# Layer-norm scaling on GpSimd, odd operand shapes for small VectorE steps, three small steps a chunk: a two-layer cross-attention block on Trainium2

## The chip, the cores and the metric

The kernel runs on one core of a Trainium2 chip. The metric is device time in microseconds (us), the median of three runs. The engines of the core are TensorE (PE, with PEld for its weight loads), VectorE (DVE), ScalarE (ACT), GpSimd (POOL) and SyncE (SP, which issues nearly all DMAs here). Each engine works through its own instructions in program order. What one engine needs of another is guarded by semaphores: an instruction that waits holds up everything behind it on its engine.

## The reference

Two transformer layers on x (4 sequences of 512 rows, 320 wide) with a context of 4 x 1601 rows, 192 wide; 20 heads of 16:

```python
def layer(x, context, heads=20):
    h1 = _ln(x, n1_g, n1_b)
    x = _attn(h1, h1, q1, k1, v1, o1_w, o1_b, heads) + x
    h2 = _ln(x, n2_g, n2_b)
    x = _attn(h2, context, q2, k2, v2, o2_w, o2_b, heads) + x
    h3 = _ln(x, n3_g, n3_b)
    a, g = jnp.split(h3 @ ff_w1 + ff_b1, 2, axis=-1)
    return a * jax.nn.gelu(g, approximate=False) @ ff_w2 + ff_b2 + x

def _ln(x, g, b):
    m = jnp.mean(x, axis=-1, keepdims=True)
    v = jnp.mean(jnp.square(x - m), axis=-1, keepdims=True)
    return (x - m) * jax.lax.rsqrt(v + EPS) * g + b
```

All is float32. There are three norms a layer for each of the four sequences, 24 in all.

## The kernel before, in words

**Units and chunks.** The work is cut into units: for each layer first self-attention, then cross-attention, for each sequence b and each group g of four heads (5 groups), and at last a feed-forward unit for each sequence. An attention unit goes over its keys in chunks of 128: 4 chunks in self-attention (512 keys), 13 in cross-attention (1601 keys). In a chunk, `main` lets PE compute the scores of four heads into PSUM banks (`st`, L1210), subtract the rows' maxima by one more matmul (L1213, from the row `m`), ACT take the exponential (L1223) into one of a ring of buffers, and, a chunk later, PE multiply with the values (`av`, L1237). ACT copies that to SBUF (L1253), and POOL adds it to the unit's output `o` (L1254), one add a chunk.

**Maxima.** The next unit's maxima are found in the same chunks: PE computes its scores once more with queries in the partitions (`sps`, L1024), and DVE reduces each bank of 512 keys to one column (L1043, `pm` or `nmax`; L1062 for the rest of the keys). `max_reduce` (L1079) joins the columns of a cross unit. `max_end` splits the 16 maxima into a rounded part and a remainder (L1089 and L1090, into the tile `nm`), transposes them on DVE (L1091) and sends them with four DMAs into the row `m`. All this shares the eight PSUM banks: a bank that DVE has not yet read holds up the matmul which is to have it next.

**Norms.** `add_norm` puts the steps of a norm into a chain. For each 128 rows t of four, `stats(t)` computes mean and variance on DVE (L530, L531) into `mv`. `root` computes the reciprocal square root of the four variances: a first guess by integer arithmetic (`guess_root`, L494 to L498 on DVE, L500 on POOL), then three Newton steps (`better_root`, L507 to L510, on POOL) in two calls. `normalise(t)` is L546: (x - mean) * rstd into `hn`, by one DVE tensor-scalar instruction with two column operands, 320 wide; in a feed-forward norm a second one, 64 wide, writes a copy of the last columns. `turn(k)` transposes `hn` on PE (L559), ACT applies gain and bias (L566), and POOL adds the bias row of the coming projection to x (L572), which may not happen before `hn` has been made from x. The first norm of all is done while `start["on"]` is true, with its root on DVE.

**What orders the work.** Chains of small jobs (norms, projections, values, splits of queries and keys) are kept in queues with costs and due times. After the matmuls of each chunk `steps` runs jobs from them. A job of cost `LIGHT` (a `stats`, the first part of `root`, a `normalise`, a transposition of context, a reciprocal) is run only while `clock["lights"]` lasts: `lights` is the number of such jobs in one call, two a chunk, or one in the last chunk of a unit and in chunks with extra maxima; one in feed-forward units. Two rounds of the clock pass in a chunk. `root` step 1, `normalise(0)` and `turn(0)` each ask for a round after the step before. `see` adds an instruction to the model by which PSUM banks are chosen (class `Pace`).

**Queries and keys.** The projected queries and keys are copied by ACT and, in cross-attention, DVE to a staging tile; POOL splits them into a rounded part and a remainder (`split`, L700 and L701), and two rounds later SP moves them to where the matmuls read them.

Of the kernel before, what the change touches and what calls it, by code (L numbers as in the profile page):

```python
# [9 lines left out]
F32 = mybir.dt.float32  # L10
F32R = mybir.dt.float32r
I32 = mybir.dt.int32
AF = mybir.ActivationFunctionType
ALU = mybir.AluOpType
# [9 lines left out]
P = 128  # L24
NQ = N // P
G, HG = 5, 4
GD = HG * DH
SLOT = 32
# [98 lines left out]
def kernel(ctx: ExitStack, tc: tile.TileContext, x, context, ws, out):  # L127
# [18 lines left out]
    nc = tc.nc  # L146
    dma = nc.sync.dma_start

    const = ctx.enter_context(tc.tile_pool(name="const", bufs=1))
# [26 lines left out]

    nmax = [const.tile([P, HG * NQ], F32, name=f"nmax{i}") for i in range(2)]
    kbuf = [const.tile([P, 4 * QT + P], F32, name=f"kT{i}") for i in range(4)]  # L180
    qbuf = [const.tile([P, 2, 2, N // 2], F32, name=f"q{i}") for i in range(4)]

# [307 lines left out]

    def guess_root(var):

        a, h, y, z = (two.tile([P, NQ], F32, tag=f"root{i}", name=f"root{i}") for i in range(4))
        see(nc.vector.tensor_scalar(a, var, EPS, None, ALU.add))  # L494
        see(nc.vector.tensor_scalar(
            z.bitcast(I32), a.bitcast(I32), 1, None, ALU.logical_shift_right
        ))
        see(nc.vector.tensor_scalar(y.bitcast(I32), z.bitcast(I32), -1, 0x5F3759DF, ALU.mult, ALU.add))  # L498
        eng = nc.vector if start["on"] else nc.gpsimd
        eng.tensor_scalar(h, a, -0.5, None, ALU.mult)  # L500
        return h, y, z
# [8 lines left out]
        eng.tensor_tensor(y, y, z, ALU.mult)  # L510

    hn_used = []


    readers = []
# [5 lines left out]
    def add_norm(l, b, i, put, done, due):  # L521
        xb = xs[b]
        s = {}

        def stats(t):
            if t == 0:
                hn_used.append(b)
                s["mv"] = two.tile([P, NQ, 2], F32, tag="mv", name="mv")
            st = three.tile([P, 6], F32, tag="st6", name="st6")
            see(nc.vector.bn_stats(st, xb[:, t, :]))  # L530
            see(nc.vector.bn_aggr(s["mv"][:, t, :], st))  # L531

        def root(step):
            if step == 0:
                s["root"] = guess_root(s["mv"][:, :, 1])
                s["rstd"] = s["root"][1]
            for _ in range(step + 1):
                better_root(*s["root"])
            s["round"] = clock["round"]

        def normalise(t):
            if t == 0:
                s["hn"] = one.tile([P, NQ, D + REST], F32, tag="hn", name="hn")

            for to, at, n in ((0, 0, D), (D, D - REST, REST))[: 1 + i // 2]:
                see(nc.vector.tensor_scalar(  # L546
                    s["hn"][:, t, to : to + n], xb[:, t, at : at + n],
                    s["mv"][:, t, 0:1], s["rstd"][:, t : t + 1], ALU.subtract, ALU.mult,
                ))
            s["round"] = clock["round"]  # L550

        def turn(k, at, n):
            if k == 0:
                s["hT"] = two.tile([P, 3, N], F32, tag="hT", name="hT")
                readers.append(done)
            ps = step_bank([P, N], "hps")
            n += REST if n == REST else 0
            for t in range(NQ):
                see(nc.tensor.transpose(ps[:n, t * P : (t + 1) * P], s["hn"][:, t, at : at + n], ident))  # L559
            if start["on"] and k == 1:  # L560
                see(nc.vector.tensor_scalar(
                    s["hT"][:n, k, :], ps[:n, :],
                    lng[i][:n, k : k + 1], lnb[i][:n, k : k + 1], ALU.mult, ALU.add,
                ))
            else:
                see(nc.scalar.activation(  # L566
                    s["hT"][:n, k, :], ps[:n, :], AF.Identity,
                    bias=lnb[i][:n, k : k + 1], scale=lng[i][:n, k : k + 1],
                ))
            for t in ((0,), (1,), (2, 3))[k]:  # L570

                nc.gpsimd.tensor_tensor(xb[:, t, :], xb[:, t, :], brow[(3 * l + i) % 2], ALU.add)  # L572
            if k == 2:
                hn_used.pop()
                put(s["hT"])

        for t in range(NQ):
            add(
                "norm", LIGHT, lambda t=t: stats(t), due - 22 + t,
                (lambda: stage[b] == 3 * l + i and not hn_used and b in loaded) if t == 0 else yes,  # L580
                (lambda: b == 0 or clock["round"] >= loaded[b] + 5) if t == 0 else yes,
            )
        for step in range(2):
            add(
                "norm", 0.0 if step else LIGHT, lambda step=step: root(step), due - 18 + step, yes,
                (lambda: clock["round"] > s["round"]) if step else yes,
            )
        for t in range(NQ):
            add(
                "norm", LIGHT, lambda t=t: normalise(t), due - 13 + t, yes,  # L590
                (lambda: clock["round"] >= s["round"] + 1) if t == 0 else yes,
            )
        for k, at, n in (DK if i < 2 else FK + [(2, 2 * P, REST)]):
            add(
                "norm", 0.58, lambda k=k, at=at, n=n: turn(k, at, n), due - 6 + 2 * k,
                may_overwrite if k == 0 else yes, lambda: clock["round"] >= s["round"] + 1,
            )
# [413 lines left out]
    def max_pairs(u):  # L1011

        full = u.nkeys // 512
        rest = u.nkeys - full * 512
        ns = full + (1 if rest else 0)
        u.nm = nmax[u.n % 2]
        u.pm = two.tile([P, NQ, HG, ns], F32, tag="pm", name="pm") if ns > 1 else None

        def passes(heads, outs, t, keys):

            def one_pass(e):
                for j, out in zip(heads, outs):
                    rows = slice(j * SLOT, (j + 1) * SLOT)
                    see(nc.tensor.matmul(  # L1024
                        out,
                        lhsT=u.q[rows, t // 2, e, t % 2 * P : (t % 2 + 1) * P].bitcast(F32R),
                        rhs=u.kT[rows, keys].bitcast(F32R),
                        start=(e == 0),
                        stop=(e == 1),
                    ))  # L1030

            return [lambda e=e: one_pass(e) for e in range(2)]

        def full_two(heads, t, s):
            pss = [bank("sps") for _ in heads]
            if ns == 1:
                to = u.nm.rearrange("p (j t) -> p j t", t=NQ)[:, :, t]
            else:
                to = u.pm[:, t, :, s]

            def reduce():
                for j, ps in zip(heads, pss):
                    see(nc.vector.tensor_reduce(to[:, j : j + 1], ps, AX.X, ALU.max, negate=(ns == 1)))  # L1043

            keys = slice(u.k0 + s * 512, u.k0 + (s + 1) * 512)
            return passes(heads, pss, t, keys), reduce

        def rest_two(heads):

            w = rest + rest % 2  # L1050
            pss = [bank("sps") for _ in heads]
            todo = [
                f
                for t in range(NQ)
                for f in passes(
                    heads, [ps[:, t * w : (t + 1) * w] for ps in pss], t, slice(u.nkeys - w, u.nkeys),
                )
            ]

            def reduce():  # L1060
                for j, ps in zip(heads, pss):
                    see(nc.vector.tensor_reduce(  # L1062
                        u.pm[:, :, j, full], ps[:, : NQ * w].rearrange("p (t w) -> p t w", w=w), AX.X, ALU.max
                    ))

            return todo, reduce

        pairs = [
            deque([lambda heads=heads, t=t, s=s: full_two(heads, t, s)] for s in range(full) for t in range(NQ))
            for heads in ((2, 3), (0, 1))  # L1070
        ]
        if rest:
            for q, heads in zip(pairs, ((2, 3), (0, 1))):
                q.append([lambda heads=heads: rest_two(heads)])
        return pairs
# [6 lines left out]

    def max_end(u):

        both = two.tile([P, SLOT], F32, tag="nm2", name="nm2")
        turned = two.tile([P, SLOT], F32, tag="turned", name="turned")
        high, low = (both.rearrange("p (j e t) -> p e j t", j=HG, e=2)[:, e] for e in range(2))
        nm = u.nm.rearrange("p (j t) -> p j t", t=NQ)
        see(nc.vector.tensor_scalar(high.bitcast(F32R), nm, 1.0, None, ALU.mult))  # L1089
        see(nc.vector.tensor_tensor(low, nm, high, ALU.subtract))  # L1090
        see(nc.vector.transpose(turned, both))  # L1091
        to = u.mrow.rearrange("(n s) (t i r) -> s i n t r", s=DH, t=NQ, r=SLOT)[0]
# [104 lines left out]
    def main(u, give, nxt):  # L1197
# [60 lines left out]
        for c in range(u.nch):  # L1258
# [15 lines left out]
                round_of([], extra[0])  # L1274
            flush()
            late.append(lambda c=c: values(c))
            steps(None, 1 if extra or c == u.nch - 1 else 2)
            for i, e in enumerate(extra[1:]):
                if i and next_cost() is not None:
                    run(pick())  # L1280
# [303 lines left out]
```

## Time and profile before

| | |
|---|---|
| median of 3 runs | 3002.72 us (3000.33 to 3009.86) |
| the profiled execution, its own time | 2998.76 us |
| span of its instructions | 2997.0 us |
| mean granted TensorE clock | 0.996 |
| POOL adds of `o` (L1254), two largest groups | 359 x 1283 ns, 191 x 1283 ns |
| maxima on DVE (L1043), two groups | 1920 x 682 ns, 640 x 682 ns |

How to read it: the page and the views of the trace give one execution. A group's row is: line, engine, operation, output and inputs by their names, shapes, count; then busy time in us and mean ns of one; then the idle time of the engine just before these instructions, with what ended it. A row with a line's instructions gives shortest, median and longest duration in ns, and first and last start. A row of the timeline begins with the start and the duration in us; in brackets stands the idle time before it. In a row of stretches the columns are the stretch, its length, the busy us (and instructions) of PE, PEld, DVE, ACT and POOL, then the granted clock, the share of DMA and its GB/s.

### The profile page before, as it was taken

How to read it: one execution, taken by the hardware profiler on the slowest of the kernel's cores; microseconds unless marked ns; L12 is line 12 of the kernel's file. 1: busy time of each engine (PE TensorE's matmuls, PEld its weight loads, DVE VectorE, ACT ScalarE, POOL GpSimd, SP SyncE). 2: the span in 40 equal slices, each digit the busy share in tenths (PEclk: the TensorE clock that was granted, in tenths of full speed). 3: DMA queues.
4: the chain of work that ended last, by engine and by line, in shares of the span. 5: the costliest groups of instructions: out<-in, count | busy, mean ns of one | idle time of the engine just before them, and what ended most of it. 6: DMA issues, size and time to landing. Idle time of an engine off the chain costs nothing. (4 is left out here: it accounts for less than half of the span.)

```text
span 2997.0 us, 92121 instructions
## 1 busy us (share of the span) xinstructions
PE 2918.5 (97%) x37842; PEld 1605.1 (54%) x37842; DVE 2054.5 (69%) x4011; ACT 1955.5 (65%) x4029; POOL 1325.0 (44%) x1499
## 2 busy tenths in 40 slices
PE   8999999999999999999999999999999999999999
PEld 4455555555555555455554555555555555544555
DVE  7777878788888788322257778788878877873221
ACT  4777577887887888511147775778878878884101
POOL 3556454555455554201125563555654554541100
PEclk9999999999999999999999999999999999999999
DMA  4434221222132121300124332221221221212000
GB/s 113 120 98 113 71 70 44 64 70 58 43 76 60 34 65 28 111 7 0 32 51 100 106 87 64 65 65 32 71 58 36 54 69 38 56 36 74 14 10 14
DMA packets 221150, 178.00 MB, mean 59 GB/s; under 512 B 137652, under 2 KB 175416, under 8 KB 220728
## 3 DMA queue, kind: packets, MB, share of 16 engines
q1 hardware_dynamic: 219928, 171.05, 22.2%
q8 instruction: 297, 4.87, 0.7%
q14 instruction: 125, 1.02, 0.1%
q10 hardware_dynamic: 800, 1.06, 0.1%
HBM read 54.67 MB, written 29.56 MB: 28 GB/s over the span
## 5 line engine op out<-in xcount | busy, mean ns | idle before, releaser
L1043 DVE TENSOR_REDUCE pm<-sps 128x1 f32<-128x512 f32 x1920 | 1191.9, 682 | 108.3 <-PE sps L1024 101.5
L1024 PE MATMUL sps<-kT,q 32*128 32x512 f32 (+1 forms) x6400 | 1059.0, 402 | 18.2 <-DMA q<-stage 6.2
L1223 ACT ACTIVATE pr<-st 128x512 f32<-128x512 f32 (+1 forms) x1710 | 904.8, 603 | 189.4 <-PE st L1213 179.5
L1210 PE MATMUL st<-q,kT 32*128 32x512 f32 (+1 forms) x5440 | 921.6, 433 | 2.9 <-DVE pm L1043 1.3
L1254 POOL TENSOR_TENSOR o<-o,pr 128x512 f32<-128x512 f32 x359 | 460.5, 1283 | 642.9 <-ACT pr L1253 632.0
L1210 PEld LDWEIGHTS st<-q,kT 32*128 32x128 f32 (+1 forms) x5440 | 476.8, 180 | 353.8 <-ACT pr L1223 142.1
L1237 PE MATMUL av<-pr,vals 128*32 128x512 f32 (+1 forms) x3420 | 635.3, 607 | 31.3 <-DVE pm L1043 8.4
L1024 PEld LDWEIGHTS sps<-kT,q 32*128 32x128 f32 x6400 | 547.6, 184 | 119.8 <-DVE pm L1043 19.2
L1213 PE MATMUL st<-m,units 32*128 32x512 f32 (+1 forms) x2720 | 529.6, 390 | 0.8 <-DMA m<-turned 0.8
L1223 ACT ACTIVATE wself<-st 128x512 f32<-128x512 f32 (+1 forms) x867 | 462.8, 603 | 83.3 <-PE st L1213 79.6
L1043 DVE TENSOR_REDUCE nmax<-sps 128x1 f32<-128x512 f32 x640 | 396.8, 682 | 124.0 <-PE sps L1024 120.2
L1237 PE MATMUL av<-wself,vals 128*32 128x512 f32 (+1 forms) x1734 | 369.7, 605 | 12.3 <-DVE pm L1043 5.3
L1254 POOL TENSOR_TENSOR o<-o,wself 128x512 f32<-128x512 f32 x191 | 245.0, 1283 | 291.7 <-ACT wself L1253 288.7
L1332 PE MATMUL fps<-hT,w 128*128 128x512 f32 x640 | 283.7, 597 | 0.0
L1355 ACT ACTIVATE pr<-fps,b 128x512 f32<-128x512 f32 x80 | 54.8, 688 | 345.9 <-PE fps L1345 245.3
L1213 PEld LDWEIGHTS st<-m,units 32*128 32x128 f32 (+1 forms) x2720 | 249.0, 180 | 19.8 <-POOL stage L700 1.2
L1253 ACT COPY pr<-av 128x512 f32<-128x512 f32 x359 | 219.0, 610 | 25.1 <-PE av L1237 24.9
L1332 PEld LDWEIGHTS fps<-hT,w 128*128 128x128 f32 x640 | 118.8, 190 | 149.4 <-issue 148.5
L1237 PEld LDWEIGHTS av<-pr,vals 128*32 128x32 f32 (+1 forms) x3420 | 91.3, 108 | 199.2 <-DVE pm L1043 109.7
L700 POOL TENSOR_SCALAR stage<-stage 128x256 fp32r<-128x256 f32 (+1 forms) x155 | 106.5, 687 | 141.3 <-ACT stage L850 75.2
L500 POOL TENSOR_SCALAR root<-root 128x4 f32<-128x4 f32 x23 | 5.2, 224 | 298.2 <-DVE root L494 298.0
L885 PEld LDWEIGHTS kps<-ctxT,w 32*128 32x128 f32 (+1 forms) x4992 | 113.2, 162 | 43.3 <-ACT pr L1223 21.2
(99 smaller groups left out, 3161.3 us busy)
## 6 DMA issues: line engine op xcount, KB each, us to landing
q<-stage SPq DMA_DIRECT2D x157, 256.0 KB
kT<-w SPq DMA_DIRECT2D x120, 208.0 KB
outs<-o SPq DMA_DIRECT2D x80, 256.0 KB
kT<-stage SPq DMA_DIRECT2D x78, 128.0 KB
aT<-outs SPq DMA_DIRECT2D x32, 224.0 KB
oturn<-over SPq DMA_DIRECT2D x32, 224.0 KB
kT<-w SPq DMA_DIRECT2D x40, 144.0 KB
w<-in_L_xattn_ff_w_dram SPq DMA_DIRECT2D x20, 256.0 KB
```

The lines of the kernel that those rows point to most:

```text
L700: eng.tensor_scalar(high.bitcast(F32R), x, 1.0, None, ALU.mult)
L885: see(nc.tensor.matmul(ps[to : to + n, :PIECE], lhsT=wk_q[rows, k, u.g * GD : u.g * GD + n], rhs=first.kvT[rows, k, at : at + PIECE], star ...
L1024: see(nc.tensor.matmul(out, lhsT=u.q[rows, t // 2, e, t % 2 * P : (t % 2 + 1) * P].bitcast(F32R), rhs=u.kT[rows, keys].bitcast(F32R), star ...
L1043: see(nc.vector.tensor_reduce(to[:, j : j + 1], ps, AX.X, ALU.max, negate=(ns == 1)))
L1210: see(nc.tensor.matmul(st[:r, :], lhsT=keys, rhs=u.q[rows, :, e].bitcast(F32R), start=(e == 0), stop=False))
L1213: see(nc.tensor.matmul(st[:r, :], lhsT=units_of[rows, :r].bitcast(F32R), rhs=u.mrow[rows, :].bitcast(F32R), start=False, stop=True,))
L1223: see(nc.scalar.activation(p[:r], st[:r], AF.Exp))
L1237: see(nc.tensor.matmul(ps[j * SLOT : (j + 1) * SLOT, :], lhsT=columns_of[:r, head : head + SLOT], rhs=pr.pop((c, j))[:r, :], start=True, s ...
L1253: see(nc.scalar.copy(vo, ps))
L1254: nc.gpsimd.tensor_tensor(u.o, u.o, vo, ALU.add)
L1332: see(nc.tensor.matmul(ps, lhsT=w1[:, k, i * FF + c * P : i * FF + (c + 1) * P], rhs=u.hT[:, k, :], start=ahead and k == 0, stop=not ahead ...
L1355: see(nc.scalar.activation(gl, pss[1], AF.Gelu, bias=b1[:, NHC + c : NHC + c + 1]))
```

## The change

`normalise` issues its instruction on POOL instead of DVE, save for the first norm, and the instruction no longer goes through `see`. The tiles of the root get other shapes: three of them are views of 3 x 2 elements in a tile of 3 x 3, the fourth is 6 elements without a gap; `mv` becomes two fixed tiles with two more columns, set to 1 once at the start. So the root is taken of six values, of which four are used. The first step of `max_end` now reads 20 elements in one row, the 16 maxima and four zeros that are set once, and writes 5 groups of 4 apart from each other, in a room 8 elements wider. `steps` is called with three light jobs a chunk where it was two. No DMA is added or taken away.

```diff
-    nmax = [const.tile([P, HG * NQ], F32, name=f"nmax{i}") for i in range(2)]
+    nmax = [const.tile([P, (HG + 1) * NQ], F32, name=f"nmax{i}") for i in range(2)]
+    for nm in nmax:
+        nc.gpsimd.memset(nm[:, HG * NQ :], 0.0)
...
-        a, h, y, z = (two.tile([P, NQ], F32, tag=f"root{i}", name=f"root{i}") for i in range(4))
+        a, h, y = (two.tile([P, 3, 3], F32, tag=f"root{i}", name=f"root{i}")[:, :, :2] for i in range(3))
+        z = two.tile([P, 6], F32, tag="root3", name="root3").rearrange("p (a b) -> p a b", b=2)
...
+    mvs = [const.tile([P, 6, 2], F32, name=f"mv{i}") for i in range(2)]
+    for mv in mvs:
+        nc.gpsimd.memset(mv[:, NQ:], 1.0)
...
-                s["mv"] = two.tile([P, NQ, 2], F32, tag="mv", name="mv")
+                mvs.reverse()
+                s["mv"] = mvs[0]
...
-                s["rstd"] = s["root"][1]
+                s["rstd"] = [s["root"][1][:, t // 2, t % 2 : t % 2 + 1] for t in range(NQ)]
...
-                see(nc.vector.tensor_scalar(
+                these = (
                     s["hn"][:, t, to : to + n], xb[:, t, at : at + n],
-                    s["mv"][:, t, 0:1], s["rstd"][:, t : t + 1], ALU.subtract, ALU.mult,
-                ))
+                    s["mv"][:, t, 0:1], s["rstd"][t], ALU.subtract, ALU.mult,
+                )
+                if start["on"]:
+                    see(nc.vector.tensor_scalar(*these))
+                else:
+                    nc.gpsimd.tensor_scalar(*these)
...
-        u.nm = nmax[u.n % 2]
+        u.nmax = nmax[u.n % 2]
+        u.nm = u.nmax[:, : HG * NQ]
...
-        both = two.tile([P, SLOT], F32, tag="nm2", name="nm2")
+        room = two.tile([P, SLOT + 2 * NQ], F32, tag="nm2", name="nm2")
+        both = room[:, :SLOT]
...
-        see(nc.vector.tensor_scalar(high.bitcast(F32R), nm, 1.0, None, ALU.mult))
+        apart = room.rearrange("p (j e t) -> p e j t", j=HG + 1, e=2)[:, 0]
+        see(nc.vector.tensor_scalar(apart.bitcast(F32R), u.nmax, 1.0, None, ALU.mult))
...
-            steps(None, 1 if extra or c == u.nch - 1 else 2)
+            steps(None, 1 if extra or c == u.nch - 1 else 3)
```

## The prediction

> **What bounds the kernel now.** I read the busy times first, then the same by stage, then who makes TensorE (PE) wait, then the groups of VectorE (DVE) and GpSimd (POOL).
>
> ```profile
> span 2997.0 us, 92121 instructions
> PE 2918.5 (97%) x37842; PEld 1605.1 (54%) x37842; DVE 2054.5 (69%) x4011; ACT 1955.5 (65%) x4029; POOL 1325.0 (44%) x1499
> ```
>
> PE is the bound: 78.5 us of the span are without a matmul. An edit on DVE and POOL can only win part of these, or add to them.
>
> ```profile
> 45.00:1209.00 1164.00, 1131.03 (x17289) 634.45 (x17288) 939.33 (x1833) 910.66 (x1902) 620.11 (x656) 1.00 0.27 68
> 1209.00:1406.00 197.00, 197.00 (x935) 98.74 (x931) 58.33 (x130) 49.01 (x83) 29.28 (x71) 1.00 0.14 43
> 1406.00:2694.00 1288.00, 1256.41 (x17983) 701.08 (x17982) 958.18 (x1838) 928.70 (x1932) 635.71 (x685) 1.00 0.23 59
> ```
>
> By stage (length, then PE, PEld, DVE, ACT, POOL busy): the first feed-forward stage has no idle PE at all. The two attention stages, 2452 us, hold 33.0 + 31.6 = 64.6 us of it. There DVE is 81% busy (939.33 of 1164) and second to PE. With 80 self and 260 cross chunks a layer, a chunk lasts about 1164 / 340 = 3.4 us.
>
> ```profile
> PE av L1237 <- DVE pm L1043: 14.0, 26, 1.3
> PE av L1237 <- DVE nmax L1043: 10.1, 19, 1.9
> PE av L1237 <- DVE pm L1062: 3.2, 2, 1.8
> ```
>
> PE's own waits (us, times, longest): with these three DVE accounts for 27.3 us. PE needs a bank that a late maximum has not yet read. What makes the maxima late:
>
> ```profile
> 1615.20 0.20 POOL L510 TENSOR_TENSOR root<-root,root 128x4 f32<-128x4 f32 x1
> 1615.36 0.86 POOL L700 TENSOR_SCALAR stage<-stage 128x256 fp32r<-128x256 f32 x1
> 1615.43 0.96 DVE L546 TENSOR_SCALAR hn<-x,mv,root 128x320 f32<-128x320 f32 x2 [1.42 <-POOL root L510]
> 1616.50 0.58 DVE L1090 TENSOR_TENSOR nm<-nmax,nm 128x16 f32<-128x16 f32 x1
> 1617.96 0.62 PE L1237 MATMUL av<-w,vals 128*32 128x512 f32 x1 [1.95 <-DVE nmax L1043]
> ```
>
> In order of time: DVE stands 1.42 us before the normalisation because POOL's root is not done, works on it, and PE then loses 1.95 us. A second cause, the lock, is in these rows:
>
> ```profile
> 507.76 1.27 POOL L1254 TENSOR_TENSOR o<-o,wself 128x512 f32<-128x512 f32 x1
> 507.84 1.37 DVE L546 TENSOR_SCALAR hn<-x,mv,root 128x320 f32<-128x320 f32 x1 [0.66 <-POOL root L510]
> 262.05 0.44 DVE L546 TENSOR_SCALAR hn<-x,mv,root 128x320 f32<-128x320 f32 x1
> ```
>
> The same normalisation takes 0.44 us, or 1.37 us if a POOL instruction has just begun: it ends 0.18 us after POOL's does (509.21 against 509.03). [...]
>
> **The change part by part.**
>
> ```profile
> L546 DVE TENSOR_SCALAR hn<-x,mv,root 128x320 f32<-128x320 f32 x96 | 55.8, 601 | 26.0 <-POOL root L510 25.9
> L546 DVE TENSOR_SCALAR hn<-x,mv,root 128x64 f32<-128x64 f32 x32 | 17.5, 548 | 0.0
> L1089 DVE TENSOR_SCALAR nm<-nmax 128x16 fp32r<-128x16 f32 x80 | 19.0, 238 | 1.5
> L1090 DVE TENSOR_TENSOR nm<-nmax,nm 128x16 f32<-128x16 f32 x80 | 15.8, 198 | 2.7
> L498 DVE TENSOR_SCALAR root<-root 128x4 int32<-128x4 int32 x24 | 9.2, 385 | 0.8
> L495 DVE TENSOR_SCALAR root<-root 128x4 int32<-128x4 int32 x24 | 4.1, 170 | 0.8
> L530 DVE BATCH_NORM_STATS2 st<-x 128x6 f32<-128x320 f32 x96 | 45.3, 472 | 1.9 <-DMA x<-in_x_dram 1.9
> L531 DVE BATCH_NORM_AGGREGATE mv<-st 128x2 f32<-128x6 f32 x96 | 17.5, 182 | 3.3
> ```
>
> *Removed from DVE.* The first of 24 norms stays on DVE. The other 23 take away about 23/24 of 73.3 us, 70 us, and with them 26 us of DVE standing still for the root. What that is worth to PE I take from the stretches in which it happens: 19 windows, from 0.5 us before the root's first step to 2.5 us after the last normalisation (two windows where the root stands apart), all attention norms after the first one's:
>
> ```profile
> 65.10:84.10 19.00, 16.80 (x198) 7.92 (x191) 17.08 (x34) 14.91 (x30) 8.45 (x20) 1.00 0.34 90
> ...
> 2427.40:2435.50 8.10, 7.38 (x112) 4.32 (x108) 7.85 (x16) 5.29 (x11) 2.90 (x4) 1.00 0.27 104
> sum 308.50, PE 285.62 PEld 153.73 DVE 249.00 ACT 190.80 POOL 152.05; mean PE 15.03 PEld 8.09 DVE 13.11 ACT 10.04 POOL 8.00
> ```
>
> PE is idle for 22.9 of these 308.5 us (7.4%), against 64.6 - 22.9 = 41.7 us in the other 2143.5 us of attention (1.9%). At the ordinary rate the stretches would lose 6.0 us; 16.9 us come on top. Lock, root wait and normalisation itself all leave DVE, so I take **-17 us**. Bounds: 0 (stats, which stay, could cause it) and the 27 us of PE's waits on DVE.
>
> *Small operands.* L495, 170 ns, never met the lock; L498 does the same kind of work in 385 on average, so 24 x 0.215 = 5.2 us of waiting. [...]
>
> ```profile
> L1089 DVE TENSOR_SCALAR nm<-nmax x80: 106/174/1141, 34.3 to 2682.5; 128x16 fp32r<-128x16 f32 x80
> L1090 DVE TENSOR_TENSOR nm<-nmax,nm x80: 174/175/581, 34.5 to 2682.7; 128x16 f32<-128x16 f32 x80
> ```
>
> Four more elements on L1089 and two more on the root: L1090 reads 16 elements from two tensors in 175 ns, so one source at single rate should not need more; I take 0 for it. Of these 10 us half lie in the stretches already counted; PE's waits on DVE are 27 us for 2054 us of DVE, hence **-1 us**, between 0 and -5. [...]
>
> *Added to POOL.*
>
> ```profile
> L572 POOL TENSOR_TENSOR x<-x,brow 128x320 f32<-128x320 f32 x96 | 83.8, 890 | 58.7 <-DVE hn L546 48.4 <-DVE stage L701 8.5
> L700 POOL TENSOR_SCALAR stage<-stage 128x256 fp32r<-128x256 f32 x75 | 64.1, 855 | 141.0 <-ACT stage L850 75.2 <-ACT stage L819 65.5 <-issue 0.2
> L700 POOL TENSOR_SCALAR w<-w 128x416 fp32r<-128x416 f32 x80 | 100.0, 1250 | 16.3 <-DVE w L895 10.9 <-DVE nm L1089 4.5 <-ACT w L895 0.7
> L500 POOL TENSOR_SCALAR root<-root 128x4 f32<-128x4 f32 x23 | 5.2, 224 | 298.2 <-DVE root L494 298.0
> L1254 POOL TENSOR_TENSOR o<-o,pr 128x512 f32<-128x512 f32 x359 | 460.5, 1283 | 642.9 <-ACT pr L1253 632.0 <-ACT vals L967 6.5 <-DMA outs<-o 2.8
> ```
>
> No row has a tensor-scalar with two column operands on POOL. Between 256 elements (855) and 416 (1250) a 320-wide one would take 1013 ns; the lower bound is L572's 890, the upper one twice the part that grows, 0.22 + 2 x 0.79 = 1.8 us. I take 1.01, and for 64 elements 224 + 60 x 2.5 = 0.37 us: 92 x 1.01 + 32 x 0.37 = 105 us on an engine that is 44% busy. No DMA moves. POOL's 299 root steps (13 for each of 23 norms, about 0.22 us each by L500) take six elements for four: 5 ns each at 2.5 ns an element, 1.5 us in all, at most half as long again, 33 us, on an engine with room for it. L572 needs no other engine now, which gives POOL back the 48.4 us for which it stood at its head.
>
> What waits for it: the transposes of L559 on PE, which can't pass their place, and behind a normalisation on POOL the o adds (L1254, one a chunk), the splits (L700) and the DMAs that need the splits. Slack is often small:
>
> ```profile
> 264.19 0.98 PE L559 MATMUL hps<-ident,hn 128*112 128x128 f32 x7
> 2434.95 0.65 PE L559 MATMUL hps<-ident,hn 128*112 128x128 f32 x4
> 2431.45 1.55 DVE L546 TENSOR_SCALAR hn<-x,mv,root 128x320 f32<-128x320 f32 x2
> 1216.91 1.98 DVE L546 TENSOR_SCALAR hn<-x,mv,root 128x320 f32<-128x320 f32 x4
> 1218.02 1.53 PE L559 MATMUL hps<-ident,hn 128*128 128x128 f32 x12
> ```
>
> At 262.05 the last normalisation begins 2.1 us before its transposes, at 2431.45 the last two 3.5 us before. These two and five more of the attention norms are about so tight. With 1.01 for 0.60 us, and each of them behind an o add, I charge 0.5 us to each, 3.5 us, and 0.75 us to the first feed-forward norm of each layer, whose transposes run while it is made (from 1218.02, with DVE at it until 1218.89): **+5 us**, between 0 and 15 attention norms x 2.5 us = 37 us (an o add, a split pair and three normalisations, 1.28 + 0.86 + 0.74 + 3.03 = 5.9 us, come 2.5 us after a chunk's end).
>
> *Three steps a chunk.* Three stats are 3 x (0.47 + 0.18) = 1.96 us of DVE in a chunk where 19% of 3.4 us, 0.65 us, is free: 0.65 us later than with two, for perhaps one chunk of a norm. Banks hide most: **+1 us**, between -2 (a norm one chunk earlier gives the transposes slack) and 15 x 0.65 = 10.
>
> Sum: -17 - 1 + 5 + 1 = **-12 us**. The profiled execution took 2998.8 us (span 2997.0), 4 us under the median of 3002.72; put on the median it is 2990.7, **2991 us**.
>
> **The rivals.** *More is won.* DVE's 26 + 70 + 10 us shorten its queue for chunks after the stretches as well, and an early norm hides POOL's slowness. Then -22 us, four fifths of the 27 us: 2981. For it: DVE is 80% busy beside PE; against: the waits outside the stretches are at the ordinary rate.
>
> *Given back.* [...] If the normalisations cost 1.2 us of PE for each of 15 norms, 18 us, all is returned: 3001, no change. [...]
>
> *Slower.* POOL's order becomes the bound: three normalisations in a row hold up the splits and the o add, the transposes and the q transfers arrive 2.5 us late at each of the 15 norms, 37 - 18 = +19 us: 3022. It decides from 1.2 us a norm on. For it: POOL is 49% busy in the stretches and its instructions are twice as long; against: it has 308.5 - 152.05 = 156 us free in them for 15 x 4.05 = 61 us more work. [...]
>
> *The odd shapes do not help.* Then the small steps keep their 10 us and 1 us is missing: 2992.
>
> **How the numbers follow.** This measurement can tell about 0.3%, 9 us, from no change: 2993.7 and 3011.7. Forecast 0.45, with its odd-shape variant 0.03 more; more won 0.16; given back 0.20; slower 0.16. Faster takes the first three less 0.02 for a forecast that falls short, 0.62; same 0.22; slower 0.16. The range runs from 2976, past the second case, to 3012, past the third.
>
> **What would show it.** L546 moves to POOL, 92 rows near 1.0 us; DVE falls to about 1950 us; L498 and L1089 have no row over 0.3 us; DVE's waits for the root are gone; PE idle falls to about 66 us. Wrong if POOL's 320-wide row is over 1.5 us, if PE waits for POOL's hn by more than 10 us, or if the maxima still keep PE as long as before.

## The result and the profile after

The changed kernel takes 3019.46 us (median of 5 runs, 3017.64 to 3020.52) against 3002.72 us: ratio 1.0053, 95% interval 1.0042 to 1.0064. It is 0.5% slower where 0.4% faster was forecast, outside the stated range, and close to the rival "slower" (3022).

The first lines of the page after:

```profile
span 3017.7 us, 92207 instructions
PE 2929.7 (97%) x37842; PEld 1615.0 (54%) x37842; DVE 1986.1 (66%) x3887; ACT 1955.7 (65%) x4029; POOL 1469.8 (49%) x1627
```

DVE has become shorter by 68 us, to 1986.1, and POOL longer by 145 us, where 105 were forecast for the normalisation. The prediction's own terms take 70 + 10 us from DVE's 2054; the "about 1950" among its signs went beyond that, and was not reached. PE without a matmul went from 78.5 to 3017.7 - 2929.7 = 88.0 us, where 66 were forecast. PE's busy time rose too, from 2918.5 to 2929.7, with the same 37842 matmuls. These two rises, 9.5 and 11.2 us, are the 20.7 us of span. (The profiled execution of before was 4 us under its median, so 4 of the 20.7 us are that.)

PE's own waits after (us in total, times, longest):

```profile
PE hps L570 <- POOL hn L560: 22.8, 16, 3.1
PE av L1251 <- DVE pm L1055: 9.4, 16, 0.9
PE av L1251 <- DVE nmax L1055: 8.6, 12, 1.7
PE sps L1036 <- DMA q<-stage: 6.5, 1, 6.5
```

The waits for maxima have shrunk from 27.3 to 18.0 us. A wait that was 0.5 us is now the largest: the transposes (`hps`) for the normalised rows (`hn`), which GpSimd now makes. GpSimd's normalisations by shape, and the small VectorE steps (shortest, median, longest in ns):

```profile
L560 POOL TENSOR_SCALAR hn<-x,mv,root 128x320 f32<-128x320 f32 x92 | 131.7, 1436 | 1.1
L560 POOL TENSOR_SCALAR hn<-x,mv,root 128x64 f32<-128x64 f32 x32 | 18.5, 580 | 0.0
L501 DVE TENSOR_SCALAR root<-root x24: 158/159/161, 6.7 to 2918.6; 128x6 int32<-128x6 int32 x24
L1103 DVE TENSOR_SCALAR nm<-nmax x80: 109/173/176, 34.7 to 2698.3; 128x20 fp32r<-128x20 f32 x80
L1104 DVE TENSOR_TENSOR nm<-nmax,nm x80: 174/176/1619, 34.9 to 2698.5; 128x16 f32<-128x16 f32 x80
L1103 DVE TENSOR_SCALAR nm<-nmax 128x20 fp32r<-128x20 f32 x80 | 13.2, 165 | 1.5
L1104 DVE TENSOR_TENSOR nm<-nmax,nm 128x16 f32<-128x16 f32 x80 | 21.0, 262 | 2.8
```

With the odd shapes L501 and L1103 have no long case any more (longest 161 and 176 ns, before 1281 and 1141). The shapes alone (run 6) bring their means to 159 and 166 ns, before 385 and 238; why the shape does this was not shown. But the neighbour with two inputs, L1104, which comes right behind L1103, now takes up to 1.62 us, before 0.58. So of the 5.8 us that left the first step of the split (19.0 to 13.2), 5.2 came back in the second (15.8 to 21.0). It is 18.6 with the shapes alone (run 6) and 18.9 with the move alone (run 7), so both have a part in it.

One of the worst places, first POOL, then PE, then the stretches around it (length; PE, PEld, DVE, ACT, POOL busy; granted clock; DMA):

```profile
1751.20 1.27 POOL L1268 TENSOR_TENSOR o<-o,pr 128x512 f32<-128x512 f32 x1 [0.15 <-ACT pr L1267]
1752.46 4.28 POOL L560 TENSOR_SCALAR hn<-x,mv,root 128x320 f32<-128x320 f32 x3
1756.72 1.25 POOL L711 TENSOR_SCALAR w<-w 128x416 fp32r<-128x416 f32 x1
1758.05 1.06 POOL L712 TENSOR_TENSOR w<-w 128x416 f32<-128x416 f32 x1
1759.07 1.26 POOL L1268 TENSOR_TENSOR o<-o,pr 128x512 f32<-128x512 f32 x1
1760.32 1.44 POOL L560 TENSOR_SCALAR hn<-x,mv,root 128x320 f32<-128x320 f32 x1
```

```profile
1758.18 0.54 PE L570 MATMUL hps<-ident,hn 128*112 128x128 f32 x3
1761.82 2.04 PE L570 MATMUL hps<-ident,hn 128*112 128x128 f32 x9 [3.10 <-POOL hn L560]
```

```profile
1760.00:1762.00 2.00, 0.18 (x2) 0.19 (x3) 0.00 (x0) 0.00 (x0) 2.00 (x3) 1.00 0.68 135
1762.00:1765.40 3.40, 3.40 (x25) 2.75 (x28) 0.34 (x1) 2.33 (x3) 3.40 (x4) 0.50 0.26 51
1765.40:1769.00 3.60, 3.60 (x64) 1.78 (x60) 2.61 (x7) 2.93 (x6) 2.35 (x4) 1.00 0.41 137
```

POOL is busy for ten microseconds with hardly a gap (the longest is 0.08 us): an o add, three normalisations, a split pair, another add, and only then the fourth normalisation. PE does three of twelve transposes and waits 3.10 us for it, with nothing to do for DVE and ACT either (0.00 busy). Then comes what the prediction did not have in its sum: for 3.40 us PE's clock is granted at 0.50. Over the whole run the granted clock fell:

```profile
core 0: 2997.0 us, clock 0.996
core 0: 3017.7 us, clock 0.989
```

(before, then after), so what the clock withheld grew from 2997.0 x 0.004 = 12 us to 3017.7 x 0.011 = 33 us.

These are two executions, and the clock differs between executions of one kernel. In 53 executions of the kernel before, run beside the experiments below, it was 0.989 to 0.996, 0.993 in the median (21 us withheld), and the time went with it: 3012.2 to 3013.2 us in the three at 0.989, 2996.6 and 2997.1 in the two at 0.996. The five executions of the changed kernel were at 0.988 to 0.990. So the usual growth is 21 to 33, 12 us; and at the same 0.989 the changed kernel (3017.6 and 3019.5 us) is still 4 to 7 us slower than the kernel before.

### The profile page after: what moved, and what is told of

It is laid out like the page before. It is cut to its first block, busy times and chain, and to the rows that moved or that the text cites. A ratio compares the mean times of both kernels' runs of the same rounds, so it can differ in the third digit from the quotient of the medians.

```text
span 3017.7 us, 92207 instructions
## 1 busy us (share of the span) xinstructions
PE 2929.7 (97%) x37842; PEld 1615.0 (54%) x37842; DVE 1986.1 (66%) x3887; ACT 1955.7 (65%) x4029; POOL 1469.8 (49%) x1627
## 5 line engine op out<-in xcount | busy, mean ns | idle before, releaser
L560 POOL TENSOR_SCALAR hn<-x,mv,root 128x320 f32<-128x320 f32 x124 | 149.2, 1215 | 1.1
```

Of the source, the lines that this page charges most:

```text
L560: nc.gpsimd.tensor_scalar(*these)
```

## The experiments

All ratios are to the kernel before, run beside each experiment on the same chip; where two experiments ran on different chips, their ratios compare better than their times. The common part of four runs is the normalisation put back on VectorE:

```diff
-                if start["on"]:
-                    see(nc.vector.tensor_scalar(*these))
-                else:
-                    nc.gpsimd.tensor_scalar(*these)
+                see(nc.vector.tensor_scalar(*these))
```

**1. Only the move undone.** The edit above alone.

> The changed kernel with the normalisation put back on VectorE; odd shapes and three steps a chunk stay. Theory (GpSimd's normalisation, 1.44 us each, comes too late for its transposes, and TensorE loses the time there): no wait of TensorE for hn over 1 us in sum, waits on VectorE's maxima come back, granted clock 0.994 or more, 2993 to 3006 us. Rival one (three steps a chunk bunch VectorE's work): time stays at 3012 or more. Rival two (GpSimd's fuller queue delays splits and adds): also near 3000, so this run does not tell it from the theory.

Measured 2991.65 us, ratio 0.9965 (0.9952 to 0.9978): faster than both kernels. Its page, waits and clock:

```profile
span 2988.9 us, 92123 instructions
PE 2920.2 (98%) x37842; PEld 1606.7 (54%) x37842; DVE 2042.9 (68%) x4011; ACT 1955.2 (65%) x4029; POOL 1328.3 (44%) x1503
```

```profile
PE av L1248 <- DVE pm L1052: 9.5, 16, 0.9
PE av L1248 <- DVE nmax L1052: 8.1, 16, 1.3
...
PE hps L567 <- DVE hn L557: 2.8, 3, 1.6
core 0: 2988.9 us, clock 0.995
```

With the other two edits in place the move thus costs 27.8 us on the medians (26 by the ratios), 28.8 on the profiles: idle PE 88.0 against 68.7 (+19.3), busy PE 2929.7 against 2920.2 (+9.5). Waits for hn explain the first (22.8 against 2.8). PE's waits for the maxima are the same with it and without (9.4 + 8.6 and 9.5 + 8.1): with the other two edits in place, the relief of DVE buys PE nothing here. The time is a little below the theory's range, and two of the theory's signs failed: PE still waits 2.8 us for hn, and the waits for the maxima did not come back. (Putting the instruction back also puts back its call of `see`; what that alone does was not run.)

**2. Two steps a chunk.**

```diff
-            steps(None, 1 if extra or c == u.nch - 1 else 3)
+            steps(None, 1 if extra or c == u.nch - 1 else 2)
```

> The changed kernel with two small steps a chunk again. Theory: the last chunk before the transposes now holds two normalisations in place of one, so the wait for hn stays or grows, 23 to 35 us of idle TensorE, 3017 to 3030 us. Rival one (the bunching of three steps costs the time): back to 3003 or less.

Measured 3024.83 us, ratio 1.0068 (1.0048 to 1.0088), within the theory's range, with a wait for hn of 22.3 us. The third step is no cause of the loss; rival one falls.

**3. The transposes one chunk later.**

```diff
-                may_overwrite if k == 0 else yes, lambda: clock["round"] >= s["round"] + 1,
+                may_overwrite if k == 0 else yes, lambda: clock["round"] >= s["round"] + 3,
```

> The changed kernel with the transposes allowed only one more chunk after the last normalisation (three rounds in place of one). Theory: the wait for hn falls from 23 us of idle TensorE to under 6, the stretches at half clock fall back to some 25 us, and what VectorE's relief is worth shows: 2972 to 2990 us. Rival two (GpSimd's queue delays splits and adds, whatever the transposes do): the wait for hn goes, and the time stays over 3003.

Measured 3010.61 us, ratio 1.0025 (1.0016 to 1.0034). The wait for POOL's hn fell to 4.7 us as expected, the time by 9 us only; the theory's 2972 to 2990 us are missed, and the clock did not recover (0.990 in the median of ten executions). What took the wait's place, in the order POOL, SP, PE:

```profile
263.90 4.28 POOL L560 TENSOR_SCALAR hn<-x,mv,root 128x320 f32<-128x320 f32 x3
268.15 0.85 POOL L711 TENSOR_SCALAR stage<-stage 128x256 fp32r<-128x256 f32 x1
269.09 0.73 POOL L712 TENSOR_TENSOR stage<-stage 128x256 f32<-128x256 f32 x1
```

```profile
269.84 1.22 SPq L838 DMA_DIRECT2D q<-stage  x2
271.49 1.43 SPq L866 DMA_DIRECT2D kT<-stage  x2
273.03 2.65 SPq L1109 DMA_DIRECT2D m<-turned  x4
```

```profile
276.88 0.50 PE L1227 MATMUL st<-m,units 32*128 32x512 f32 x2 [3.73 <-DMA m<-turned]
```

Three normalisations stand ahead of a split of the queries; SP's first transfer begins as the split ends (269.82), and behind it on the same queue wait the keys and the row of maxima `m`, which needs nothing of GpSimd: DVE had finished it at 265.54. PE waits 3.73 us for that row. So rival two is at work as well: not only the transposes pay. Against run 1 PE idles 13.9 us more (82.6 against 68.7), and the rows of its waits name it: the row `m` 8.9 against 1.5, the maxima 21.5 against 17.6, hn 7.0 against 2.8 (the first norm's on DVE counted in).

**4. One operation in GpSimd's normalisation.** This kernel leaves out the product with rstd on GpSimd, and with it the second column operand; it serves for its time alone.

```diff
-                    nc.gpsimd.tensor_scalar(*these)
+                    nc.gpsimd.tensor_scalar(*these[:3], None, ALU.subtract)
```

> The changed kernel with one arithmetic operation in GpSimd's normalisation: x minus mean, the product with rstd left out there (all norms but the first). If the price goes by operation, the 320-wide one takes 0.95 to 1.1 us, the wait for hn falls to about half, 11 us, and the time to 2995 to 3010. If it goes by the column operands or is the same for any tensor-scalar, it stays over 1.3 us and the time over 3015.

Measured 2999.07 us, ratio 0.9983 (0.9973 to 0.9993).

```profile
L560 POOL TENSOR_SCALAR hn<-x,mv 128x320 f32<-128x320 f32 x92 | 99.2, 1086 | 0.0
```

With one operation 1086 ns, near the 1013 of the prediction; the second operation with its column operand is what costs the other 350 (which of the two is not told apart). The wait for hn halves to 11.4 us and the time falls by 20 us. So even near the forecast price the whole change is 0.17% faster (0.07 to 0.27), short of the 0.4% forecast.

**5, 6, 7. Each edit alone on the kernel before**: three steps; odd shapes (the changed kernel with the normalisation on VectorE and two steps); the move.

```diff
-            steps(None, 1 if extra or c == u.nch - 1 else 2)
+            steps(None, 1 if extra or c == u.nch - 1 else 3)
```

> The kernel before with three small steps a chunk and nothing else. Both edits together, with the normalisation on VectorE, won 11 us. Theory A (the odd shapes win them, the third step little): 2998 to 3004 us. Theory B (the third step wins them, since norms run ahead sooner): 2989 to 2996.

> The kernel before with the odd, unequal shapes of root and maxima and nothing else: normalisation on VectorE, two steps a chunk. Theory A: 2991 to 2997 us, with no root step or split of the maxima over 0.3 us. Theory B: 2998 to 3004.

> The kernel before with the normalisation on GpSimd and nothing else. With the odd shapes and two steps a chunk the move gave 3024.8 us. If the odd shapes are worth their 3 to 8 us with the move too, 3026 to 3034 us; the transposes wait 20 us or more of idle TensorE for hn. If the shapes matter only beside a normalisation on VectorE, 3020 to 3026.

Measured: three steps alone 2996.30 us, ratio 0.9973 (0.9960 to 0.9987); odd shapes alone 3000.34 us, 0.9980 (0.9968 to 0.9992); the move alone 3027.92 us, 1.0070 (1.0049 to 1.0090). Theory A falls: the odd shapes' time is within theory B's range, the third step's 0.3 us above it, and the third step wins about as much as the odd shapes or more. The intervals of the two overlap, so which one is worth more is not settled. The move alone is in its first range by time; but its ratio, 1.0070, is that of run 2, 1.0068, which differs by the odd shapes: beside the move they win nothing that shows. PE's waits with the move alone:

```profile
PE hps L563 <- POOL hn L553: 22.3, 15, 3.0
PE av L1241 <- DVE pm L1047: 16.6, 25, 1.9
PE av L1241 <- DVE nmax L1047: 7.4, 17, 1.0
```

Against the three rows of before, 14.0 + 10.1 + 3.2 = 27.3 us, the move leaves 24.0: it relieves PE of 3.3 us of waits for maxima there, and adds 22.3. With every row of 0.2 us or more in which PE waits for DVE's maxima or for its sums to x, the relief is 8 us (33.3 to 25.3).

**8. An odd shape for the normalisation itself.** As run 1, with the 16 attention norms writing three rows of 112 at a pitch of 113 from 336 elements in a row (the tile of x is 16 columns longer, set to 0).

```diff
+                see(nc.vector.tensor_scalar(
+                    s["hn"][:, t, : 3 * PITCH].rearrange("p (k w) -> p k w", w=PITCH)[:, :, : PITCH - 1],
+                    xflat[b][:, t * D : t * D + 3 * (PITCH - 1)],
+                    s["mv"][:, t, 0:1], s["rstd"][t], ALU.subtract, ALU.mult,
+                ))
```

> Normalisation on VectorE with an odd, unequal shape of its own in the 16 attention norms (336 elements in a row, 16 of them not used, written as 3 rows of 112 at a pitch of 113), odd shapes of the small steps and three steps a chunk as in the run at 2991.65 us. If the lock is what makes the normalisation take 0.44 to 1.4 us, all attention ones take 0.45 to 0.60 us and none over 0.7, and the time is 2983 to 2990. If the lock costs TensorE nothing that shows, the time stays at 2990 to 2994.

Measured 2992.45 us, ratio 0.9949 (0.9929 to 0.9969), the same as run 1 within the intervals. All 64 took 581 to 626 ns: none is long any more (in run 1 the longest normalisation took 1531 ns), but none takes the 0.44 us of an undisturbed one either, and the mean (614 ns) is that of the same 64 in run 1 (620 ns). So the long cases, which the prediction calls the lock, cost TensorE nothing that shows, as against a duration that is always the same; what 64 normalisations at 0.44 us would win was not measured.

**9. The wait filled.**

```diff
+            if k == 0 and not start["on"]:
+                for _ in range(8):
+                    nc.tensor.matmul(ps[:, :P], lhsT=ident, rhs=ident, start=True, stop=True)
```

> The changed kernel with eight matmuls of 128 x 128 that need nothing of the norm ahead of the transposes of every norm but the first, about 1 us a norm, 23 us in all; 16 of these norms have TensorE standing there for 1.4 us on average, so the work lies in the wait there and costs some 7 us in the others. If the waits at the transposes are what brings TensorE's clock to half afterwards, the stretches at half clock fall from 70 us to 45 or less and the time is 3008 to 3020 us. If the half clock comes from elsewhere, they stay at 60 or more and the time is 3022 to 3032.

Measured 3031.66 us, ratio 1.0093 (1.0078 to 1.0108): the time is the rival's, since the added matmuls took twice what was allowed for (46.7 us for 23, in 368 records for 184 matmuls):

```profile
L571 PE MATMUL hps<-ident 128*128 128x128 f32 x368 | 46.7, 280 | 0.0
PE hps L573 <- POOL hn L560: 9.0, 9, 1.6
core 0: 3032.6 us, clock 0.993
```

46.7 us of work made the span 14.9 us longer, so 31.8 us were found elsewhere: 13.8 in the wait for hn (22.8 to 9.0). The clock rose from 0.989 to 0.993, which is 33 to 21 us withheld, 12 us more; 6 us are not assigned. At half clock 21 us withheld are 42 us of stretches, under the theory's 45; and all four executions were at 0.993 to 0.997, where the changed kernel was at 0.988 to 0.990. That the half clock follows from PE standing still at the transposes is borne out, since nothing else was changed. Run 3 shows that it does not follow from these waits alone: there they were nearly gone, and the clock was still 0.990.

**10. Two and two.** The first two normalisations of a norm on GpSimd, the last two on VectorE.

```diff
-                if start["on"]:
+                if start["on"] or t > 1:
```

> The changed kernel with the first two normalisations of a norm on GpSimd and the last two on VectorE. If the price is that the last one comes too late for the transposes, their wait falls to under 8 us of idle TensorE and the time to 2990 to 3000 us. If the price is GpSimd's load as such, or the lock between the two engines (the last two still have the even shape), the time stays at 3003 to 3012.

Measured 2983.11 us, ratio 0.9931 (0.9911 to 0.9951): the fastest of all, below the range of the theory.

```profile
span 2983.9 us, 92149 instructions
PE 2917.7 (98%) x37842; PEld 1607.6 (54%) x37842; DVE 2018.6 (68%) x3949; ACT 1953.5 (65%) x4029; POOL 1400.0 (47%) x1565
```

```profile
PE av L1251 <- DVE pm L1055: 10.4, 20, 0.9
...
PE av L1251 <- DVE nmax L1055: 6.4, 12, 1.2
...
PE hps L570 <- DVE hn L558: 1.1, 1, 1.1
PE hps L570 <- POOL hn L560: 0.9, 2, 0.5
```

The wait for hn is 2.0 us in all, 0.9 of it for GpSimd. The time is 8.5 us under run 1, and the intervals of the two ratios just do not overlap. The same instruction on the same engine hardly costs PE anything when what it makes is not needed next. Half the normalisations were also taken from GpSimd's queue, so this run does not tell the late transposes from the late transfers; but a price that goes by GpSimd's load would have left half of the loss, not a gain.

**11. Four steps a chunk**, as run 1 with 4 for 3.

> Normalisation on VectorE, odd shapes, and four small steps a chunk in place of three. Two to three was worth 8 us without the odd shapes. If norms that run ahead sooner keep paying, 2980 to 2988 us; if three was enough (a norm has four steps of a kind and its parts wait for each other by chunks), 2989 to 2996; if bunching starts to cost, over 2997.

Measured 3003.32 us, ratio 1.0006 (0.9995 to 1.0016), in the range expected if bunching costs: what three steps won is gone with four.

**12. The chain earlier.** The transposes as in run 3, and the first normalisation allowed in the chunk of the root.

```diff
-                (lambda: clock["round"] >= s["round"] + 1) if t == 0 else yes,
+                (lambda: clock["round"] >= s["round"]) if t == 0 else yes,
```

> The changed kernel with GpSimd's normalisations allowed in the chunk of the root (both are on GpSimd, in order) and the transposes in the chunk where they stand in the changed kernel, so one more chunk lies between. If lateness at the transposes is the whole price, their wait falls under 8 us of idle TensorE and, unlike the run with later transposes, nothing else moves: 2985 to 3000 us. If what the move costs is GpSimd's load (splits, adds, transfers late), the time stays at 3005 or more.

Measured 3023.74 us, ratio 1.0063 (1.0042 to 1.0084). The time is in the range of the rival, GpSimd's load; the wait for POOL's hn was 11.7 us, more than expected, and the row `m` was late once more:

```profile
275.64 0.50 PE L1227 MATMUL st<-m,units 32*128 32x512 f32 x2 [3.62 <-DMA m<-turned]
```

An earlier leave to start does not make GpSimd's work shorter. Why this version is 13 us slower than run 3 stays open; its wait for hn is 7 us longer.

## Why the prediction was wrong, point by point

**"-17 us" for taking the normalisation off VectorE** is the first step that failed. It put down to the move all the idle PE that the stretches around a norm hold above the ordinary rate. The runs show a relief of 3.3 to 8 us of PE's waits for the move alone (run 7), and none once shapes and third step are in (18.0 against 17.6 us). The stretches hold the root steps, the split of the maxima and the stats too, and the other two edits brought the waits for maxima down without the move (27.3 to 17.6 us in run 1). A stretch in which several things coincide does not price one of them. The lower bound, 0, was the right end.

**"I take 1.01"** for a 320-wide normalisation on GpSimd was under-sized: 1.436 us measured, between the bounds of 0.89 and 1.8. The rows it was read from have one operation and no column operand; this instruction has two of each. On VectorE the same instruction takes 0.44 us (the four of the first norm). Still, VectorE is the better place here only against all four pieces of a norm on GpSimd (run 1, 2991.65 us against 3019.46), not against two of the four (run 10, 2983.11).

**"+5 us"** for late transposes: the mechanism was right, the size was not. The waits alone are 22.8 us, more than four times that and within its bounds of 0 to 37. Of the prediction's signs of being wrong this one came true: PE waits for hn by more than 10 us. The slack was judged by one normalisation's longer duration; on the engine stand an add, splits and up to three normalisations in a row, as the rival "slower" had it.

**A term was missing**: PE's clock. About 12 us more are withheld in the changed kernel than usually in the one before (33 against 21; 21 more in the two profiled executions), and 18 more than in the profiled execution of run 1 (2988.9 x 0.005 = 15). Part of this falls into waits, so it does not add to the time in full; the rise of PE's busy time by 9.5 us from run 1 is what certainly does.

**"-1 us" for the shapes** and **"+1 us" for the third step**: 0.9980 and 0.9973 of before measured on the kernel before, some 6 and 8 us of gain each, together 11 in run 1. Each matters more to PE than the counts of microseconds on DVE suggested: its waits for the maxima fell to 22.6 and 23.5 us. Of the 10 us of waiting behind the "-1", 5.2 are the root's step; the rest, put on the split's first step, no run shows by itself. With the shapes alone (run 6) the root's step lost 5.4 us of DVE (9.2 to 3.8) and the split's first one 5.7 (19.0 to 13.3), while its second gained 2.8 (15.8 to 18.6). Without the move the sign of the third step was wrong too, and its bound of -2 too narrow. Beside the move less is shown: nothing for the shapes (run 2 against run 7), and for the third step 1.0068 against 1.0053, with overlapping intervals.

**The rival "slower"** had the mechanism (GpSimd's order), the main place (the transposes) and nearly the time, 3022, from 2.5 us a norm. Its second place, the q transfers, hardly pays in the changed kernel (PE's wait for q is 6.5 us, before 6.2); late transfers show in runs 3 and 12. In fact the price is 1.0 us of wait a norm (22.8 over 23) with the clock behind it. That its time came so near is luck: a price more than twice too high was set against 18 us of gain which were not there, and "it decides from 1.2 us a norm" rested on the same gain.

**"Given back"** was right in its outcome that nothing is won by moving all. The runs give order as the reason; for the lock, the long cases of 1.37 us against 0.44, there is only the 3.1 us of DVE by which L1104 grows with the move alone (15.8 to 18.9), and run 8, where the long cases of the normalisation went and nothing was won. Run 10 shows that moving half does help.

## What to carry to other kernels

When work goes to a slower engine, price the last piece before its reader, behind everything that stands ahead of it on that engine's queue, and not the mean; here two of four pieces moved were worth 8 us and four of four cost 28. Price an instruction by its number of operations and column operands, from a row that has as many (on GpSimd 1436 ns with two of each, 1086 with one). A stall on TensorE can cost more than its length: behind the wait of 3.10 us came 3.40 us at a granted clock of 0.50. So read the granted clock beside the idle time, and over several executions, since it differs between executions of one kernel.

## What the runs showed of the hardware

A GpSimd tensor-scalar of 128 x 320 takes 1436 ns with two operations and two column operands, and 1086 with one of each; VectorE does the former in 439 to 446 ns (the four that the changed kernel leaves there).

Half clock came behind waits shorter than those 3.10 us too. At this place of the changed kernel waits of 0.64 and 2.33 us, with 0.32 us of matmul between them, came ahead of 3.40 us at a granted clock of 0.50 (the second wait, then stretches):

```profile
2018.02 1.32 PE L570 MATMUL hps<-ident,hn 128*112 128x128 f32 x5 [2.33 <-POOL hn L560]
```

```profile
2015.00:2018.00 3.00, 0.32 (x1) 0.13 (x1) 0.38 (x2) 0.11 (x1) 3.00 (x4) 1.00 0.03 5
2018.00:2021.40 3.40, 3.38 (x25) 2.41 (x25) 0.86 (x2) 1.95 (x3) 2.85 (x3) 0.50 0.02 2
```

The 3.00 us ahead of this stretch held 0.32 us of busy PE. It is as long as the one at 1762.00, 3.40 us; what sets that length was not shown.
